# The projection's bias on VectorE, and the output's row sums from its last additions

## The chip, the core and the metric

The kernel runs on one core of one Trainium2 chip. The core has five engines that work side by side, each through its own list of instructions in a fixed order: TensorE (PE) multiplies matrices, VectorE (DVE) and ScalarE (ACT) do elementwise work and are the ones that carry matrix products out of PSUM, GpSimd (POOL) does elementwise work between SBUF tiles, and SyncE (SP) issues transfers. The metric is device time in microseconds (us) of one execution; smaller is better. Three runs of the kernel before took 2961.35, 2961.88 and 2963.93 us, so the median is 2961.88 us.

## The reference

Four graph layers, each followed by a layer norm of the sum of its input and its output, over 128 batches of 128 nodes with 512 features, all in 32-bit floats. The change is in layer 3, masked attention with eight heads, a projection with bias, and an inner layer norm:

```python
o = jnp.einsum('bhnm,bhmd->bhnd', attn, v).transpose(0, 2, 1, 3).reshape(b, n, d)
o = o @ w_proj + b_proj
mu = jnp.mean(o, axis=-1, keepdims=True)
var = jnp.mean(jnp.square(o - mu), axis=-1, keepdims=True)
ln = (o - mu) * jax.lax.rsqrt(var + LN_EPS) * ln_gamma + ln_beta
return o + ln
...
x = _layernorm(x + _L3_gnn_ref(x, ...), axis=-1)
```

So for each row the kernel needs `o` with its bias, the sum of `o` over the row (for the mean) and the sum of its squared deviations.

## The kernel before

**The planner.** The order of all engines' instructions is computed while the kernel is built. Each batch, and each product, is a Python generator (a chain) that asks for an engine with an estimated duration (`use("ACT", 0.48, ...)`), and `Plan.run` gives the engines out, one request at a time, by the earliest possible start, then by the request's order (`urgent`, `follow`) and the chain's rank, which mostly is the batch's number. `Plan.use` multiplies a duration by its engine's entry in `SLACK`. Instructions are issued in the order in which the planner grants them. A different duration, engine or constant anywhere therefore moves instructions of all engines against each other, in the whole kernel. The order of the instructions is fixed by this; the real start of each is fixed by semaphores on the chip.

**Buffers.** One arena of 100 units of 256 columns holds all the large tiles. A request can ask for a slot of a kind (`t` two units, `v`, `qk` and `xT` four). `CAPS` limits how many slots of a kind may be held at once: `xr`, the rows of x fetched again for the final sum, and `xT`, the transposed input of the layer-3 sections, are among them. The eight PSUM banks are handed out in the same way.

**Seven products for eight.** Large products of two blocks by two blocks are done by `seven` with seven block products (a Strassen-Winograd scheme). It accumulates on one PSUM bank `x`: after each step the partial sum is taken out to SBUF (`kept`), and the next matmul adds to the same bank, so TensorE cannot go on with this bank until the copy is done. The planner puts other matmuls in between. `kept` takes three partial sums out to where they are finished (ACT copies, line 943), `added` adds other banks onto them (DVE, `total`, line 937, or line 931 with `into`, which also writes the row sums through `accum_out`), and `last` takes out the fourth block (ACT, line 1025). In the inner section (`inner_section`, matmuls on line 892) `kept` adds on DVE instead (lines 950 and 952). `pair_product` (matmuls on line 1058) uses `seven` on pairs of batches: layer 0 with `into`, layer 1 without, and the projection of layer 3 (`projection`) without. `section` (matmuls on line 1111) uses it for q, k and v.

**The end of a batch.** After attention (`attends`, line 1212) ACT copies the heads' output (line 1457), and `projection` runs for two batches at a time, all but the last four batches. Then, for each batch, POOL adds the bias to the whole of `o` (`pool_add`, line 386, called on line 1468); `normed` has POOL add `o` to the fetched x (line 1540), ACT goes over `o` once to get its row sum (line 1560, `accum_out`), `statistics` turns the sum into the negative mean (DVE, line 357), the squared deviations (ACT, line 364) and the reciprocal root (POOL, line 321), and DVE makes the layer norm and the sum of the output (lines 1571 and 1576). The last `ENDS` = 8 batches take mean and variance with DVE's `bn_stats` (`mean_rstd`, line 308) instead. Batches before the last `KEPT` = 8 write x to DRAM (`spill`, line 1230) and fetch it again (`fetch`, line 1238), both through SP.

**The softmax.** Eight exponentials for each batch on ACT, one for each head (line 1407, each with an accumulator read); in the last `WHOLE` = 3 batches one ACT instruction over all heads instead (line 1401), with a subtraction and a sum on DVE beside it (lines 1397 and 1403).

Of the kernel before, what the change touches and what calls it, by code (L numbers as in the profile page):

```python
# [8 lines left out]
F32 = mybir.dt.float32  # L9
AF = mybir.ActivationFunctionType  # L10
ALU = mybir.AluOpType
# [4 lines left out]
P = 128  # L16
D = 512
K = D // P
G = 4
APART = 4  # L20
FIRST = 0
PAIRS = 2
SOON = (-4, 8, -4, 6, 10, 12)
WHOLE = 3
KEPT = 8
ATTENDS = 2
RUN = 5
SEVEN0 = 1
# [4 lines left out]
WAKE = 0.1  # L33
SWIFT = 0, 1, 2, 3, 4, 5
BEGIN = 1
ENDS = 8
INNER = 3
SEVEN1 = 1
SEVENP = 1
# [2 lines left out]
STICK = 0.6  # L42
CLOSE = 2900
SOFT = 8
PROJ = -3
SECTION = 22
PACE = 0
EAGER = 8
H = 8
# [7 lines left out]

UNITS = 100
UNIT = 256
CAPS = {"x": 8, "xr": 2, "yT": 11, "v": 5, "qk": 11, "xT": 6}  # L60
SIZES = {"u": 1, "t": 2, "x": 2, "early": 2, "xr": 2, "yT": 2, "v": 4, "qk": 4, "xT": 4}
LAST, AHEAD = 26, 0
DIRECT = 22
LATER = 2
LANDED = 2.2
LATE = 1.4
HANDOFF = {"PE": 0.2, "DVE": 0.13, "ACT": 0.16, "POOL": 0.09, "SP": 0.05}
DVE_ = 1.02
ACT_ = 1.08
POOL_ = 1.02  # L70
SP_ = 1.2
SLACK = {"PE": 1.0, "DVE": DVE_, "ACT": ACT_, "POOL": POOL_, "SP": SP_}
BORDERS = 0.1
# [170 lines left out]
def gnn_stack_kernel(  # L244
# [89 lines left out]

    def row_sums():

        n = small.tile([P, 6], F32, name="sums", bufs=20)
        return [n[:, c : c + 1] for c in range(6)]

    def layernorm_sums(xb, total, unread, pieces=1, total_out=None):  # L340
# [341 lines left out]
    class Group:  # L682


        def __init__(self, first, size):
            self.first, self.size, self.half = first, size, size // 2
            self.s = small.tile([P, G, 2], F32, name="s")
            self.logits = [Event(2) for _ in range(size // 2)]
            self.attention = [Event() for _ in range(size // 2)]
            self.landed, self.qk = Event(size), Event(8)  # L690
            self.have = {t: Event() for t in (T1, T2, T3, T4)}
            self.inner = {t: Event() for t in (I1, I2, I3, I4)}
            self.used = {t: Event(3) for t in (B11, B21)}
            self.squared = [Event() for _ in range(size)]
            self.valued = [Event(2) for _ in range(2)]
            self.rows, self.attended, self.scored = ([Event() for _ in range(size)] for _ in range(3))
            self.heads, self.o, self.sc, self.scratch = {}, {}, {}, {}
            self.eT, self.xT, self.slot, self.left = {}, {}, {}, {}
            self.qkT, self.v = {}, {}
            self.y, self.y_slot, self.mixed, self.turned, self.h = {}, {}, {}, {}, {}  # L700
            self.y0, self.mixed0, self.added0, self.biased, self.total = {}, {}, {}, {}, {}
            self.begun = [Event() for _ in range(3)]
            self.wide, self.dropped = Event(), Event()
            self.copied = [Event(2) for _ in range(size // 2)]
            self.projected = [[Event(2) for _ in range(2)] for _ in range(size // 2)]
            self.p, self.extra = [{} for _ in range(size // 2)], {}

        def block(self, t):

# [209 lines left out]
            adds=True, blocks=(B11, B21, B22, I1, I2, I3, I4),  # L919
        )  # L920

    def seven(rank, bx, wide, time, multiply, parts, finished, have, home, housed, slow=0.0, into=None, scale=None, adds=False, inner=None,
              blocks=(B11, B21, B22, T1, T2, T3, T4)):

        b11, b21, b22, t1, t2, t3, t4 = blocks
        copy, sum_ = {D: (0.45, 0.6), D // 2: (0.24, 0.33), P: (0.14, 0.2)}[wide]
        copy, sum_ = copy + slow, sum_ + slow

        def total(a, c, i, j):
            if into:  # L930
                nc.vector.scalar_tensor_tensor(  # L931
                    c, a, 1.0, c, op0=ALU.mult, op1=ALU.add, accum_out=into[j][i]
                )
            elif scale:
                nc.vector.scalar_tensor_tensor(c, a, scale, c, op0=ALU.mult, op1=ALU.add)
            else:
                nc.vector.tensor_tensor(c, a, c, op=ALU.add)  # L937

        def copied(c, a):
            if scale:  # L940
                nc.scalar.activation(c, a, AF.Identity, scale=scale)
            else:
                nc.scalar.copy(c, a)  # L943

        def kept(p, i, j, event):
            if into or adds:
                yield use("DVE", sum_, urgent=True)
                for a, c in parts(p, i, j):
                    if scale:
                        nc.vector.scalar_tensor_tensor(c, a, scale, c, op0=ALU.mult, op1=ALU.add)  # L950
                    else:
                        nc.vector.tensor_tensor(c, a, c, op=ALU.add)
                done(event)
                return
            got = yield use("ACT", copy, lambda: home(j), urgent=True)
            if got:
                housed(j, got)
            for a, c in parts(p, i, j):
                copied(c, a)
            done(event)  # L960

        def keep(p, i, j):
            event = Event()
            plan.start(kept(p, i, j, event), rank)
            return event

        def added(p, kept, i, j, event):
            yield kept
            yield use("DVE", sum_, urgent=True)
            for a, c in parts(p, i, j):  # L970
                total(a, c, i, j)
            finished(j)
            done(event)

        def add(p, kept, i, j):
            event = Event()
            plan.start(added(p, kept, i, j, event), rank)
            return event

        def release(event, bank):  # L980
            yield event
            give(bank)

        x = bank(bx, D)[:, :wide]
        multiply(x, A11, b11, True)
        m1 = keep(x, 0, 0)

        if inner:
            plan.start(inner(m1), rank)
        else:  # L990
            bz = yield use("PE", time, "ps")
            z = bank(bz, D)[:, :wide]
            multiply(z, A12, b21, True, True)
            plan.start(release(add(z, m1, 0, 0), bz), rank)

        yield m1
        yield have[t2]
        yield use("PE", time)
        multiply(x, S2, t2)
        u2 = keep(x, 1, 0)  # L1000

        yield have[t3]
        by = yield use("PE", time, "ps")
        y = bank(by, D)[:, :wide]
        multiply(y, S3, t3, True)
        yield u2
        yield have[t1]
        yield use("PE", time)
        multiply(x, S1, t1)
        u4 = keep(x, 1, 1)  # L1010
        c22 = add(y, u4, 1, 1)
        yield u4
        yield use("PE", time)
        multiply(x, S4, b22, final=True)

        def last(bx):
            if into or adds:
                yield use("DVE", sum_, urgent=True)
            else:
                yield use("ACT", copy, urgent=True)  # L1020
            for a, c in parts(x, 0, 1):
                if into or adds:
                    total(a, c, 0, 1)
                else:
                    copied(c, a)
            give(bx)
            finished(1)

        plan.start(last(bx), rank)
        yield c22  # L1030
        yield have[t4]
        yield use("PE", time)
        multiply(y, A22, t4, final=True)
        plan.start(release(add(y, u2, 1, 0), by), rank)
# [10 lines left out]
            nc.gpsimd.tensor_tensor(blocks(out), blocks(a), blocks(b), op=ALU.subtract)  # L1045
            done(have[t])

    def pair_product(rank, s, ready, blocks, release, out, finished, differed=None, into=None):

        yield ready  # L1050
        have = {t: Event() for t in (T1, T2, T3, T4)}
# [26 lines left out]
        def housed(j, slot):  # L1078
# [1 line left out]

        bx = yield use("PE", 0.87, "ps")
        yield from seven(
            rank, bx, D // 2, 0.87, multiply, parts, finished, have, home, housed, into=into,
        )

    def section(gr, s, before):
# [154 lines left out]
    def batch(i):  # L1241
# [218 lines left out]
        if SEVENP and gr.first + 2 * h < NB - PLAIN:  # L1460
            if h not in gr.extra:
                gr.extra[h] = None
                plan.start(projection(gr, h, i + PROJ), i + PROJ)
            done(gr.copied[h])
            yield gr.projected[h][b % 2]
            o, slot = gr.p[h][b % 2], gr.p[h]["slot", b % 2]
            biased = Event()
            plan.start(pool_add(o, bproj_sb, biased), i)
            yield biased
            yield from normed(i, o, lambda: give(slot), fetched)  # L1470
        else:
            yield from (last if i == NB - 1 else usual)(
                i, oT, v, lambda: gr.read(("v", b // 2), 2), fetched
# [35 lines left out]
    def projection(gr, h, i):  # L1509
# [20 lines left out]
        if gr.first + 2 * h + 2 == NB - PLAIN:  # L1530
            plan.start(again(), 0)
        yield from pair_product(
            i, 4, gr.copied[h], lambda t: t3 if t == T3 else v[:, t], release, gr.p[h],
            lambda j: done(gr.projected[h][j]), differed,
        )

    def add_rows(o, fetched, i):
# [12 lines left out]
        give(bp)  # L1550
        yield from normed(i, o, release, fetched)

    def normed(i, o, release, fetched):

        added = yield from add_rows(o, fetched, i)
        xb = xs[i]
        if i < NB - ENDS:
            total = row_sums()
            slot = yield use("ACT", 0.72, "t")
            nc.scalar.activation(buf(slot, D), o, AF.Identity, accum_out=total[0])  # L1560
            give(slot)
            nm, rstd, mean = yield from statistics(o, total, None)
            yield use("DVE", 0.07, urgent=True)
            nc.vector.tensor_scalar(mean, nm, -(D**0.5), None, op0=ALU.mult)
        else:
# [120 lines left out]
```

## Time and profile before

The profiled execution took 2960.8 us, with a span of 2959.0 us from the first to the last instruction, at a mean granted TensorE clock of 0.998.

| what | value |
|---|---|
| median of three runs | 2961.88 us |
| profiled execution, its span | 2960.8 us, 2959.0 us |
| ACT busy | 2052.8 us (69%) |
| POOL busy | 1894.8 us (64%) |
| DMA, mean over the span | 144 GB/s |
| PE busy, 100 to 2900 us, lowest and highest 100 us | 98.11 and 100.00 us |
| DVE busy, 100 to 2900 us, lowest and highest 100 us | 74.30 and 92.77 us |
| ACT copies of 128x256 on line 943 | 768, mean 368 ns |
| DVE adds of 128x256 on line 937 | 514, mean 414 ns |
| ACT row sums on line 1560 | 120, mean 623 ns, and 192 ns for each accumulator read |

An instruction count and a mean in a row of the profile cover one line and one shape. "Idle before" is the time in which the engine stood still just before instructions of the row, with the instruction that ended most of it. Matmul records are modelled at their ends: a 128x256 matmul is listed with 380 ns, though eight of them follow each other in 1.73 us, so a busy PE hides gaps shorter than the overlap.

### The profile page before, as it was taken

How to read it: one execution, taken by the hardware profiler on the slowest of the kernel's cores; microseconds unless marked ns; L12 is line 12 of the kernel's file. 1: busy time of each engine (PE TensorE's matmuls, PEld its weight loads, DVE VectorE, ACT ScalarE, POOL GpSimd, SP SyncE). 2: the span in 40 equal slices, each digit the busy share in tenths (PEclk: the TensorE clock that was granted, in tenths of full speed). 3: DMA queues.
4: the chain of work that ended last, by engine and by line, in shares of the span. 5: the costliest groups of instructions: out<-in, count | busy, mean ns of one | idle time of the engine just before them, and what ended most of it. 6: DMA issues, size and time to landing. Idle time of an engine off the chain costs nothing. (4 is left out here: it accounts for less than half of the span.)

```text
span 2959.0 us, 57327 instructions
## 1 busy us (share of the span) xinstructions
PE 2927.7 (99%) x17061; PEld 2476.9 (84%) x17061; DVE 2502.2 (85%) x7410; ACT 2052.8 (69%) x6211; POOL 1894.8 (64%) x2128
## 2 busy tenths in 40 slices
PE   9999999999999999999999999999999999999998
PEld 5688888888888888888888888888888888888886
DVE  7999888879888888888888788988878888878778
ACT  4657776667767577676767677677675786767675
POOL 4765757576666675665766666776666666666555
PEclk9999999999999999999999999999999999999999
DMA  6235745465455554554555465555446555544344
GB/s 221 83 90 154 191 118 172 109 183 131 128 159 152 148 158 118 162 149 127 169 129 164 115 172 144 160 150 152 132 130 177 141 145 152 148 123 122 107 140 128
DMA packets 861846, 425.40 MB, mean 144 GB/s; under 512 B 551008, under 2 KB 765024, under 8 KB 861536
## 3 DMA queue, kind: packets, MB, share of 16 engines
q1 hardware_dynamic: 843104, 388.18, 48.3%
q10 hardware_dynamic: 18432, 33.56, 3.0%
q8 instruction: 137, 2.24, 0.3%
q14 instruction: 173, 1.42, 0.2%
HBM read 219.68 MB, written 201.92 MB: 142 GB/s over the span
## 5 line engine op out<-in xcount | busy, mean ns | idle before, releaser
L1045 POOL TENSOR_TENSOR arena<-arena 128x256 f32<-128x256 f32 (+1 forms) x848 | 747.3, 887 | 383.9 <-ACT arena L1457 123.4
L321 POOL TENSOR_TENSOR sums<-sums,neghalf 128x1 f32<-128x1 f32 x631 | 417.8, 668 | 445.6 <-DVE sums L369 362.7
L943 ACT COPY arena<-ps 128x256 f32<-128x256 f32 (+1 forms) x892 | 340.8, 397 | 312.1 <-PE ps L1111 183.4
L1058 PE MATMUL ps<-wsum_sb,arena 128*128 128x256 f32 x2148 | 527.4, 380 | 3.3 <-ACT arena L943 1.9
L1058 PE MATMUL ps<-w_sb,arena 128*128 128x256 f32 x1872 | 462.6, 380 | 0.1
L1058 PEld LDWEIGHTS ps<-wsum_sb,arena 128*128 128x128 f32 x2148 | 398.9, 190 | 74.8 <-issue 14.6
L364 ACT ACTIVATE arena<-arena,sums 128x512 f32<-128x512 f32 x481 | 345.2, 718 | 130.3 <-DVE sums L357 84.3
L937 DVE TENSOR_TENSOR arena<-ps,arena 128x256 f32<-128x256 f32 (+2 forms) x824 | 315.1, 395 | 130.5 <-ACT arena L943 56.0
L1058 PEld LDWEIGHTS ps<-w_sb,arena 128*128 128x128 f32 x1872 | 346.1, 190 | 61.2 <-issue 16.5
L1407 ACT ACTIVATE arena<-arena,nmx 128x128 f32<-128x128 f32 x1000 | 391.1, 394 | 3.2 <-DVE nmx L1393 1.6
L1111 PE MATMUL ps<-arena,wqkv_sb 128*128 128x256 f32 (+1 forms) x1616 | 365.1, 371 | 0.0
L1111 PE MATMUL ps<-arena,wsum_sb 128*128 128x256 f32 (+1 forms) x1584 | 359.8, 373 | 0.0
L1111 PEld LDWEIGHTS ps<-arena,wqkv_sb 128*128 128x128 f32 x1616 | 293.7, 190 | 41.4 <-issue 4.8
L1111 PEld LDWEIGHTS ps<-arena,wsum_sb 128*128 128x128 f32 x1584 | 287.6, 190 | 43.1 <-issue 8.6
L347 ACT ACTIVATE arena<-arena,sums 128x512 f32<-128x512 f32 x255 | 205.1, 810 | 66.6 <-DVE sums L344 55.6
L1058 PE MATMUL ps<-wproj_sb,arena 128*128 128x256 f32 x992 | 236.1, 382 | 0.0
L386 POOL TENSOR_TENSOR arena<-arena,bproj_sb 128x512 f32<-128x512 f32 x124 | 159.7, 1302 | 111.6 <-ACT arena L943 102.8
L386 POOL TENSOR_TENSOR arena<-arena,beta_sb 128x512 f32<-128x512 f32 x128 | 174.5, 1370 | 79.3 <-DVE arena L1368 63.0
L1294 DVE SCALAR_TENSOR_TENSOR arena<-arena,wa_rows 128x512 f32<-128x512 f32 x256 | 210.3, 826 | 5.0 <-PE ps L1111 2.3
L1058 PEld LDWEIGHTS ps<-wproj_sb,arena 128*128 128x128 f32 x992 | 185.4, 190 | 28.9 <-issue 1.1
L1422 ACT ACTIVATE arena<-arena,rs 128x128 f32<-128x128 f32 x512 | 194.1, 396 | 5.2 <-DVE rs L1414 1.8
L1407 ACT ACTIVATION_READ_ACCUMULATOR arena<-arena,nmx 128x1 f32 x1000 | 191.0, 191 | 0.0
(143 smaller groups left out, 6026.2 us busy)
## 6 DMA issues: line engine op xcount, KB each, us to landing
p_d<-arena SPq DMA_DIRECT2D x256, 256.0 KB
arena<-p_d SPq DMA_DIRECT2D x128, 512.0 KB
x_d<-arena SPq DMA_DIRECT2D x234, 256.0 KB
arena<-x_d SPq DMA_DIRECT2D x936, 64.0 KB
arena<-in_x SPq DMA_DIRECT2D x127, 256.0 KB
out<-arena ACTq DMA_DIRECT2D x127, 256.0 KB
x_s<-arena SPq DMA_DIRECT2D x120, 256.0 KB
arena<-x_s SPq DMA_DIRECT2D x120, 256.0 KB
```

The lines of the kernel that those rows point to most:

```text
L321: nc.gpsimd.tensor_tensor(rstd, ve, neghalf, op=ALU.pow)
L347: nc.scalar.activation(xb, xb, AF.Identity, bias=nmr, scale=rstd)
L364: nc.scalar.activation(buf_or_bank(unread), xb, AF.Square, bias=nm, scale=D**-0.5, accum_out=var)
L386: nc.gpsimd.tensor_tensor(dst, dst, other, op=ALU.add)
L937: nc.vector.tensor_tensor(c, a, c, op=ALU.add)
L943: nc.scalar.copy(c, a)
L1045: nc.gpsimd.tensor_tensor(blocks(out), blocks(a), blocks(b), op=ALU.subtract)
L1058: nc.tensor.matmul(p, t[:, k], w[:, k, :], start=first and k == 0, stop=final and k == 1, skip_group_check=True,)
L1111: nc.tensor.matmul(to, lhs, rhs, start=first and j == 0 and k == 0, stop=final and k == 1, skip_group_check=True,)
L1294: nc.vector.scalar_tensor_tensor(unread, xb, 1.0, wa_rows[:, j, :], op0=ALU.mult, op1=ALU.mult, accum_out=gr.s[:, b, j : j + 1],)
L1407: nc.scalar.activation(pr[:, j, :], pr[:, j, :], AF.Exp, bias=nmx[:, j : j + 1], accum_out=sums[:, j : j + 1],)
L1422: nc.scalar.activation(pr[:, j, :], pr[:, j, :], AF.Identity, scale=rs[:, j : j + 1])
```

## The change

1. `seven` and `pair_product` take a `bias`, and `projection` passes `bproj_sb`. In `kept`, the three partial sums of a projection are now taken out by DVE, which adds the bias on the way, and no longer copied by ACT; `last` adds the bias on DVE too.
2. `projection` also passes `into`: the additions that finish a block write the row sums of its half through `accum_out`. `normed` gets these two half sums (`total`), and `statistics` adds them (line 359 before, `pieces` = 2).
3. POOL's pass over `o` for the bias, and ACT's pass over `o` for the row sum, are gone for the batches with a paired projection. `ENDS` is gone: all these batches use the sums, and only those that are not projected in pairs use `bn_stats`.
4. Constants of the planner: `APART` 4 to 5 (how many groups at the end schedule their attention product on its own), `WHOLE` 3 to 4, `KEPT` 8 to 6, `PROJ` -3 to -4 and `SECTION` 22 to 24 and `LATER` 2 to 3 (ranks), `LAST` 26 to 22 (without effect while `AHEAD` is 0), `CAPS` of `xr` 2 to 5 and of `xT` 6 to 5, the duration factors `DVE_` 1.02 to 1.04 and `POOL_` 1.02 to 1.06, and 24 buffers for `sums` where there were 20.

```diff
-APART = 4
+APART = 5
-WHOLE = 3
-KEPT = 8
+WHOLE = 4
+KEPT = 6
-ENDS = 8
-PROJ = -3
-SECTION = 22
+PROJ = -4
+SECTION = 24
-CAPS = {"x": 8, "xr": 2, "yT": 11, "v": 5, "qk": 11, "xT": 6}
+CAPS = {"x": 8, "xr": 5, "yT": 11, "v": 5, "qk": 11, "xT": 5}
-LAST, AHEAD = 26, 0
+LAST, AHEAD = 22, 0
-LATER = 2
+LATER = 3
-DVE_ = 1.02
+DVE_ = 1.04
-POOL_ = 1.02
+POOL_ = 1.06
...
-        n = small.tile([P, 6], F32, name="sums", bufs=20)
+        n = small.tile([P, 6], F32, name="sums", bufs=24)
...
+        def half_bias(i):
+            return bias[:, i * D // 2 : (i + 1) * D // 2]
+
-        def total(a, c, i, j):
+        def total(a, c, i, j, b=None):
             if into:
                 nc.vector.scalar_tensor_tensor(
-                    c, a, 1.0, c, op0=ALU.mult, op1=ALU.add, accum_out=into[j][i]
+                    c, a, 1.0, c if b is None else b, op0=ALU.mult, op1=ALU.add, accum_out=into[j][i]
                 )
...
-            if into or adds:
+            if into and bias is None or adds:
...
-            got = yield use("ACT", copy, lambda: home(j), urgent=True)
+            got = yield use(
+                *("ACT", copy) if bias is None else ("DVE", sum_), lambda: home(j), urgent=True
+            )
             if got:
                 housed(j, got)
             for a, c in parts(p, i, j):
+                if bias is not None:
+                    nc.vector.tensor_tensor(c, a, half_bias(i), op=ALU.add)
+                    continue
                 copied(c, a)
...
-                    total(a, c, 0, 1)
+                    total(a, c, 0, 1, None if bias is None else half_bias(0))
...
+                gr.sums[h] = [row_sums() for _ in range(2)]
+                gr.osum[h] = [(n[0], n[5]) for n in gr.sums[h]]
...
-            biased = Event()
-            plan.start(pool_add(o, bproj_sb, biased), i)
-            yield biased
-            yield from normed(i, o, lambda: give(slot), fetched)
+            yield from normed(i, o, lambda: give(slot), fetched, gr.sums[h][b % 2])
...
-            lambda j: done(gr.projected[h][j]), differed,
+            lambda j: done(gr.projected[h][j]), differed, into=gr.osum[h], bias=bproj_sb,
...
-    def normed(i, o, release, fetched):
+    def normed(i, o, release, fetched, total=None):
...
-        if i < NB - ENDS:
-            total = row_sums()
-            slot = yield use("ACT", 0.72, "t")
-            nc.scalar.activation(buf(slot, D), o, AF.Identity, accum_out=total[0])
-            give(slot)
-            nm, rstd, mean = yield from statistics(o, total, None)
+        if total:
+            nm, rstd, mean = yield from statistics(o, total, None, 2)
```

More of the change, by code (lines that the diff above doesn't have):

```diff
@@ L706, in __init__ @@
             self.p, self.extra = [{} for _ in range(size // 2)], {}
+            self.sums, self.osum = {}, {}
         def block(self, t):
@@ L920, in inner_section, with seven @@
         )
-    def seven(rank, bx, wide, time, multiply, parts, finished, have, home, housed, slow=0.0, into=None, scale=None, adds=False, inner=None,
+    def seven(rank, bx, wide, time, multiply, parts, finished, have, home, housed, slow=0.0, into=None, scale=None, adds=False, inner=None, bias=None,
               blocks=(B11, B21, B22, T1, T2, T3, T4)):
@@ L1046, in differences, with pair_product @@
             done(have[t])
-    def pair_product(rank, s, ready, blocks, release, out, finished, differed=None, into=None):
+    def pair_product(rank, s, ready, blocks, release, out, finished, differed=None, into=None, bias=None):
         yield ready
@@ L1082, in pair_product @@
         yield from seven(
-            rank, bx, D // 2, 0.87, multiply, parts, finished, have, home, housed, into=into,
+            rank, bx, D // 2, 0.87, multiply, parts, finished, have, home, housed, into=into, bias=bias,
         )
```

## The prediction

> **What bounds the kernel now.** I read the page first, then the chain of waits, then the waits by engine, and last the windows of 100 us. Busy times on the page:
>
> ```profile
> PE 2927.7 (99%) x17061; PEld 2476.9 (84%) x17061; DVE 2502.2 (85%) x7410; ACT 2052.8 (69%) x6211; POOL 1894.8 (64%) x2128
> ```
>
> PE is the bound, but matmul ends are modelled, so I count its work by its cadence. The chain of waits, here from 2600 to 2700 us (start, duration, what), runs almost wholly along PE:
>
> ```profile
> 2617.91 1.72 PE ps L420 x4
> 2640.40 1.73 PE ps L1111 x8
> 2642.99 1.99 PE ps L1191 x32
> 2644.98 3.64 PE ps L1212 x64
> 2662.89 1.78 PE ps L401 x16
> ```
>
> That gives 0.216 us for a matmul of 256 columns, 0.43 for 512, 0.111 for 128, and 0.062 and 0.057 for the two of attention. Times the counts of the groups by shape (9,532, 668, 2,726, 2,048 and 2,048) this is 2059 + 287 + 303 + 127 + 117 = 2893 us. The last matmul starts 2946 us into the span; what follows is batch 127's norm and store. So PE is off its cadence for at most 2946 - 2893 = 53 us, less some 10 us of small groups (the transposes at the start, the very last product): 43 us. How much of this is waiting for another engine stands in PE's waits (engine, line, what it waited for, us, times, longest):
>
> ```profile
> PE ps L1058 <- ACT arena L943: 1.9, 5, 0.5
> PE ps L1111 <- ACT arena L943: 1.9, 1, 1.9
> PE ps L393 <- ACT arena L1457: 1.8, 1, 1.8
> PE ps L393 <- ACT arena L412: 1.6, 1, 1.6
> PE ps L892 <- DVE arena L950: 1.4, 3, 0.7
> PE ps L892 <- DVE arena L952: 1.3, 4, 0.8
> PE ps L892 <- DVE sums L357: 1.3, 4, 0.6
> ...
> PE ps L1058 <- POOL arena L1045: 0.6, 1, 0.6
> ```
>
> All seventeen rows together are 17.8 us: ACT ends 8.2 of them (with 1.0 at L1348), DVE 6.8, POOL 2.0 (1.4 of it the identity at the start), DMA 0.8. That is all that a change off PE can win. The reader should see how small it is, and that the inner section (L892) pays most of DVE's part.
>
> **The change, part by part.** PE's list holds 8,544 entries in both programs, in the same shapes, so its work does not change. The other engines, by the order of the instructions of the two programs:
>
> ACT loses 248 copies of 128x256 out of PSUM (769 become 521) and 120 row sums. 248 x 0.368 = 91 us, 120 x (0.623 + 0.192) = 98 us. `WHOLE` turns eight exponentials of (0.394 + 0.191) into one of 1.06: -3.6; four batches that now use sums instead of `bn_stats` add one pass of squares each, 4 x 0.91 = +3.6. Sum -189: ACT goes from 2053 to 1864 us (63%).
>
> POOL loses its bias pass, 124 instructions, 159.7 us: 1895 to 1735 us (59%). The pass stood in the way of nothing but the output:
>
> ```profile
> L386 POOL TENSOR_TENSOR arena<-arena,bproj_sb 128x512 f32<-128x512 f32 x124 | 159.7, 1302 | 111.6 <-ACT arena L943 102.8
> ```
>
> The only instruction that waited for it is ACT's L1560, 0.2 us in all, so taking it off the output's latency is worth nothing on the end.
>
> DVE gains 186 `kept` adds with the bias; this form stands in the trace once the last batch is reached (0.41 us, shown below), so 186 x 0.414 = +77. It gains 62 `last` adds with a row sum, not in this shape with the bias in the trace; bounds are the same add without a sum, 0.414, and the add with a sum of layer 0 (L931), 0.415 + 0.082; I take the second, +31 (low end +26). 186 adds get an accumulator read: 186 x 0.083 = +15. Adding two half sums (L359, 0.202) in place of scaling one (L357, 0.142): 120 x 0.06 = +7. `WHOLE` +2.4, fewer `bn_stats` -2.1. Sum +131: DVE goes to 2633 us, 89% of the span. It gets something back. A DVE instruction with two SBUF inputs is sometimes held for as long as a POOL pass lasts:
>
> ```profile
> L1571 DVE SCALAR_TENSOR_TENSOR arena<-arena,sums,gamma_sb x120: 705/751/1808, 327.5 to 2896.0; 128x512 f32<-128x512 f32 x120
> 2946.91 0.41 DVE L1614 TENSOR_TENSOR arena<-ps,bproj_sb 128x256 f32<-128x256 f32 x1
> ```
>
> Minimum, median and maximum are 705, 751 and 1808 ns, against a mean of 904. Means over medians at L1294, L1571, L1576 and L1335 come to some 37 + 18 + 19 + 14 = 88 us, and the bias pass is about a tenth of POOL's two-input work (159.7 of some 1,500 us): -9 us. DVE also stood 7.9 us for L1560's sums and 36.2 us at adds of this shape for ACT copies; 186 of these 514 adds, 13 us, now follow an instruction of DVE itself. So 131 us of new work stand against some 30 us less of being held.
>
> One rule speaks against this. The Trainium skill (VectorE: DVE Perf Modes, Rules for kernel authors) says to minimise the number of DVE instructions, because fusing saves nothing in itself. The order has 250 DVE instructions more (6,659 to 6,909), and 371 fewer on ACT; the rule alone would price this as a loss of DVE time, and the row above agrees in sign (0.414 us on DVE for 0.368 on ACT). It would make the sum positive only if DVE set the time.
>
> Does it? Windows of 100 us (PE, PEld, DVE, ACT, POOL busy):
>
> ```profile
> 100.00:200.00 100.00, 98.28 (x456) 74.53 (x455) 92.77 (x313) 59.62 (x145) 68.41 (x76) 1.00 0.39 103
> 1800.00:1900.00 100.00, 99.53 (x566) 84.48 (x565) 90.51 (x276) 71.28 (x212) 72.34 (x83) 1.00 0.56 155
> 2700.00:2800.00 100.00, 100.00 (x680) 88.61 (x679) 74.30 (x198) 65.97 (x211) 53.23 (x63) 1.00 0.37 104
> ```
>
> The projections begin at 319 us (the first bias pass), so 131 us over 2600 us are 5 us per 100: 90.5 becomes 95.5. The fullest window, before 200 us, has no projection. So DVE does not run out anywhere, and PE at a DVE of 90.5 is 99.5% busy. That is the cover; if it is gone, the rival below is the price.
>
> Moved steps. `KEPT` = 6 adds two x_s writes and two reads of 256 KB: 4 issues of 0.39 us, 1.6 us of SP, and 1 MB on 425. SP stands 510 us for L1426 alone, so they are hidden; without that cover, 1.6 us behind which p_d reads of the last batches wait. `xr` 5 lets rows come earlier, `xT` 5 for 6 can make a `gather` wait for a slot. No PE wait on x_d is in the trace, and PE's waits at L1111 are 1.9 us; I take 0, between -1.9 and the rival's +15. In the tail the order has attention of 126 and 127 apart and each copied with nothing left to cover it, for 1.2 us each (0.58 of copy, two handoffs); now one such wait of 1.97 us is there. +0.4, taken as 0.
>
> Covers on one PSUM bank. Between an accumulation step and the next on its bank, the order leaves less than 1.2 us of PE work 48 times in projections, now 21; in inner products 57, now 46; layers 0 and 1, 31 and 32. Projections lose nothing at theirs now (no row of it), inner products some 0.07 us for each: -0.8.
>
> **Sum.** ACT-ended waits: bounds 0 and -6.6 (without 1.6 at the start); ACT has 21% more idle time and the copies in question are part of what leaves, so I take -5. POOL-ended -0.6. Covers -0.8. DVE-ended waits: bounds -6.8 and, if they grow as its idle time shrinks (457 to 326 us), +2.7; the less blocking and the greater load pull apart, I take 0. Sum -6.4 on the profiled 2960.8, so 2954.4; the median of the runs stood 1.1 above this execution, so 2955.5, given as 2955.
>
> **The rivals.** *Hidden anyway* (0.15): PE's 99% is untouched, ACT and POOL were not the bound, and the new order has its own waits of the same size: 2961.9, within 4. For it: the waits are scattered, most under 0.8 us. Against it: ACT's are the largest. *DVE takes over the waits* (0.25): inner steps (L950, L952) queue behind new DVE adds, in each of 31 groups. The waits at L892 average some 0.36 us; one more of 0.5, a new DVE add with its sum, in each group is +15.5: 2977, and from 0.2 a group on it eats the gain. It decides once DVE is late by more than the inner step's cover, whose median in the order is 2.2 us. For it: DVE at 89%, and PE's DVE-ended waits are nearly all there. Against it: stages at 90.5 lose little. *All named waits go*: 2961.9 - 16 = 2946, the edge of the forecast.
>
> **The numbers.** About 0.2%, 5.9 us, is what a measurement of this kernel can tell from no change. Forecast 0.60, own range 2946 to 2960: 0.45 of it below 2956, 0.15 within. Hidden anyway 0.15, all within. DVE 0.25, of it 0.23 slower. So faster 0.45, same 0.32, slower 0.23. The range 2945 to 2972 takes in all but the upper half of the DVE rival and the far edge of the forecast.
>
> **What would show it.** PE's waits after should lack most rows that end in ACT L943; DVE busy near 2620, ACT near 1864, POOL near 1735; the last matmul near 2940 us. L892's rows by DVE grown past 15 us would show the rival, and PE waiting for x_d landings the `xT` cap. A time under 2943 would mean that PE's unnamed gaps moved too, which I leave out.

## The result and the profile after

The changed kernel takes 2969.03 us (median of ten runs, 2967.90 to 2972.25), the kernel before in the same session 2961.61 (ten runs, 2959.61 to 2963.93). The ratio is 1.0029 [1.0021, 1.0038]: 0.29% slower, outside the 0.2% that can be told from no change. The forecast was 2955 and faster, so its sign was wrong; the time lies inside the range.

In the listings after, lines have moved by a few: 1058 is now 1066, 1111 is 1119, 1191 is 1199, 892 stays, 401 is 400, 420 is 419, 931 is 934, 937 is 940, 952 is 955, 943 is 946, 357 is 356 (one sum) or 358 (two half sums), 386 is 385, 1571 is 1574. New is 965, the three kept partial sums of a projection, taken out by DVE with the bias. The page's busy times:

```profile
PE 2931.8 (99%) x17061; PEld 2477.8 (83%) x17061; DVE 2560.6 (86%) x7908; ACT 1907.1 (64%) x5716; POOL 1710.4 (58%) x2004
```

PE has the same 17,061 records, and ACT and POOL are lighter by 146 and 184 us. DVE is heavier by 58. The chain of waits still runs along PE, and its cadence is the old one (start, duration, what):

```profile
2607.51 1.73 PE ps L1119 x8
...
2617.01 0.86 PE ps L419 x2
...
2626.49 1.99 PE ps L1199 x32
```

Eight matmuls of 256 columns still take 1.73 us and 32 of attention 1.99. What changed is PE's waits (engine, line, what it waited for, us, times, longest):

```profile
PE ps L1066 <- DVE arena L965: 4.8, 6, 1.6
PE ps L1356 <- ACT arena L349: 3.7, 7, 1.3
PE ps L892 <- DVE arena L955: 3.5, 5, 1.3
PE ps L1602 <- ACT arena L1465: 2.2, 1, 2.2
PE ps L892 <- DVE sums L368: 1.8, 3, 0.9
PE ps L571 <- POOL ident masks.py:199: 1.4, 1, 1.4
PE ps L1119 <- POOL arena L1053: 1.3, 2, 1.0
PE ps L1066 <- DVE arena L955: 1.2, 2, 0.9
```

All rows together are 25.7 us, where they were 17.8. DVE ends 14.0 of them (6.8 before), ACT 8.8 (8.2), POOL 2.7 (2.0), DMA 0.2 (0.8). The new add of line 965 is the largest row; the steps of line 955 pay 4.7 in two rows (3.5 in the inner section, 1.2 in layer 0), where line 952 paid 1.7 before (1.3 and 0.4). By the matmul that waits, DVE's part rose at the pair products (0.4 to 7.0) and hardly in the inner section, L892 (5.4 to 5.6). The rows that end in the copies of the large products shrank as forecast, and others that end in ACT came in their place (L349, L1465).

The profiled execution of the changed kernel took 2972.25 us, the slowest of its ten, so compare its stages and not its length. Its last matmul starts 2958.4 us into the span, 12.4 us later than before; 12.1 us follow it (12.9 before), so what follows the last matmul is not the place. Against the cadence (0.216, 0.43 and 0.1115 us for matmuls of 256, 512 and 128 columns, 0.062 and 0.057 in attention) the starts of all matmuls leave 57.4 us of gaps, 45.1 before: those of at least 0.18 us sum to 31.2 us (23.9 before), shorter ones to 18.2 (15.5), and those around attention to 8.0 (5.6). So some six tenths of the 12.4 us lie in gaps of the length of the named waits. Stages of 100 us (PE, PEld, DVE, ACT, POOL busy, then granted clock, DMA share, GB/s):

```profile
100.00:200.00 100.00, 97.13 (x450) 73.60 (x449) 92.06 (x291) 59.16 (x143) 68.99 (x76) 1.00 0.39 102
600.00:700.00 100.00, 99.55 (x600) 87.35 (x599) 93.95 (x294) 74.67 (x238) 59.22 (x66) 1.00 0.56 153
2700.00:2800.00 100.00, 99.70 (x667) 85.90 (x666) 80.43 (x241) 62.08 (x192) 53.55 (x65) 1.00 0.45 124
```

DVE's fullest stage stands at 93.95, and PE is 99.55% busy in it. No engine has run out: the loss is a handful of single events. One of them, with the records of DVE, POOL and PE around it (start, duration, what; in brackets idle before):

```profile
2181.00 0.42 DVE L965 TENSOR_TENSOR arena<-ps,bproj_sb 128x256 f32<-128x256 f32 x1
...
2181.78 1.27 POOL L385 TENSOR_TENSOR arena<-arena,bias_sb 128x512 f32<-128x512 f32 x1
...
2181.83 1.49 DVE L788 SCALAR_TENSOR_TENSOR arena<-arena 128x256 f32<-128x256 f32 x1
...
2183.25 0.68 DVE L1359 TENSOR_REDUCE mx<-ps 128x1 f32<-128x512 f32 x1
...
2184.21 0.42 DVE L965 TENSOR_TENSOR arena<-ps,bproj_sb 128x256 f32<-128x256 f32 x1
...
2184.68 0.70 PE L1066 MATMUL ps<-wsum_sb,arena 128*128 128x256 f32 x2 [1.62 <-DVE arena L965]
```

Line 788 is a two-input instruction of DVE with a median of 0.42 us. Here it starts 0.05 us after a POOL pass of 128x512 and ends 0.27 us after it, 1.07 us longer than its median. The reduction behind it follows late, then the add of line 965, and PE, which needs the bank that this add frees, stands for 1.62 us. Before the change the same kind of step was a copy in ACT's queue and did not stand behind DVE's instructions.

### The profile page after: what moved, and what is told of

Same layout as the page of the kernel before. It is cut to its first block, busy times and chain, and to the rows that moved or that the text cites. A ratio compares the mean times of both kernels' runs of the same rounds, so it can differ in the third digit from the quotient of the medians.

```text
span 2970.5 us, 57212 instructions
## 1 busy us (share of the span) xinstructions
PE 2931.8 (99%) x17061; PEld 2477.8 (83%) x17061; DVE 2560.6 (86%) x7908; ACT 1907.1 (64%) x5716; POOL 1710.4 (58%) x2004
## 3 DMA queue, kind: packets, MB, share of 16 engines
q14 instruction: 173, 1.42, 0.2%
## 4 chain that ended last, share of the span: by engine, by line
PE 82%; DVE 12%; issue 1%; DMA 1%; POOL 1%; ACT 1%; SPq 0%; ACTq 0%; DVEq 0%; POOLq 0%
PE ps L1066 30%; PE ps L1119 29%; PE ps L400 4%; PE ps L1199 4%; PE ps L892 4%; PE ps L1220 4%; PE ps L1356 3%; PE ps L419 2%; PE ps L392 2%; DVE arena L934 1%; DVE arena L1434 1%; DVE arena L1424 1%; DVE arena L1579 1%; DVE arena L1574 1%; DVE nmx L1401 1%
## 5 line engine op out<-in xcount | busy, mean ns | idle before, releaser
L1053 POOL TENSOR_TENSOR arena<-arena 128x256 f32<-128x256 f32 (+1 forms) x848 | 736.3, 873 | 501.4 <-PE ps L1066 136.7
L1066 PE MATMUL ps<-wsum_sb,arena 128*128 128x256 f32 x2148 | 533.9, 381 | 6.1 <-DVE arena L965 4.8
L946 ACT COPY arena<-ps 128x256 f32<-128x256 f32 (+1 forms) x644 | 250.0, 409 | 363.7 <-PE ps L1119 203.4
L1415 ACT ACTIVATE arena<-arena,nmx 128x128 f32<-128x128 f32 x992 | 385.1, 391 | 27.7 <-DVE nmx L1401 26.0
L1066 PEld LDWEIGHTS ps<-w_sb,arena 128*128 128x128 f32 x1872 | 346.7, 191 | 58.7 <-issue 12.7
L940 DVE TENSOR_TENSOR arena<-ps,arena 128x256 f32<-128x256 f32 (+2 forms) x638 | 239.0, 388 | 114.9 <-ACT arena L946 50.4
L385 POOL TENSOR_TENSOR arena<-arena 128x512 f32<-128x512 f32 x129 | 169.1, 1316 | 132.2 <-DVE arena L934 124.5
L1430 ACT ACTIVATE arena<-arena,rs 128x128 f32<-128x128 f32 x512 | 184.2, 392 | 9.0 <-DMA arena<-x_d 3.0
```

The costliest lines, as they stand in the source:

```text
L385: nc.gpsimd.tensor_tensor(dst, dst, other, op=ALU.add)
L1066: nc.tensor.matmul(p, t[:, k], w[:, k, :], start=first and k == 0, stop=final and k == 1, skip_group_check=True,)
L1415: nc.scalar.activation(pr[:, j, :], pr[:, j, :], AF.Exp, bias=nmx[:, j : j + 1], accum_out=sums[:, j : j + 1],)
L1430: nc.scalar.activation(pr[:, j, :], pr[:, j, :], AF.Identity, scale=rs[:, j : j + 1])
```

## The experiments

The suspects, all of which would show as waits ended by DVE:

- **A**: adds on DVE make PE wait, in whatever order the work runs.
- **B**: the retuned constants are the worse part.
- **C**: every new order draws its own scattered waits, and the order of before is a low draw.
- **D**: steps that free PSUM queue behind DVE instructions that a POOL pass holds; copies on ACT do not.
- **E**: it is the sums, not the bias.

Two kinds of kernel are used. In some, the planner makes a new order. In the others ("old plan", "new plan") what the planner books is left untouched, and only the instruction issued at a booked place differs, so TensorE's list and order are exactly those of the base kernel. Ratios are to the kernel before, run in the same session.

### Code alone, constants alone

```diff
-APART, WHOLE, KEPT, PROJ, SECTION, LATER = 5, 4, 6, -4, 24, 3
+APART, WHOLE, KEPT, PROJ, SECTION, LATER = 4, 3, 8, -3, 22, 2
...
-DVE_, POOL_, CAPS xr, xT = 1.04, 1.06, 5, 5
+DVE_, POOL_, CAPS xr, xT = 1.02, 1.02, 2, 6
```

This is the code-alone kernel against the changed one, with the assignments and the two `CAPS` entries put together here; the other kernel is the kernel before with the opposite edit.

> The changed code with all planner constants of before. Theory A (the adds on VectorE make TensorE wait, whatever the order): about +7 us on before, ratio 1.002 to 1.004, and PE's waits that DVE ends near 14 us as in the changed kernel. Theory B (the retuned constants made a worse order, the code itself costs nothing): within 2 us of before, and DVE-ended waits near 7 us. Theory C (every new order draws its own waits): anywhere between -5 and +12 us, not at the same value as the changed kernel.

> The code of before with the new planner constants; ACT copies and POOL's bias pass stay. Theory A: within 2 us of before. Theory B: +7 us, as the changed kernel. Theory C: anywhere between -5 and +12 us.

Measured: code alone 2974.96 us, 1.0046 [1.0033, 1.0058]; constants alone 2979.44, 1.0058 [1.0044, 1.0072]. Each half is slower than both together (1.0029), so the two do not add, and neither is the culprit. The second is the more telling one: it has the old code, with ACT's copies, and PE's waits rose from 17.8 to 31.8 us, 19.3 of them ended by DVE, mostly at steps that the change never touched:

```profile
PE ps L892 <- DVE arena L952: 5.8, 11, 0.8
PE ps L892 <- DVE sums L357: 3.2, 5, 1.1
```

More waits ended by DVE thus come from a new order alone.

### The old plan with the new instructions

```diff
             for a, c in parts(p, i, j):
+                if bias is not None:
+                    nc.vector.tensor_tensor(c, a, half_bias(i), op=ALU.add)
+                    continue
                 copied(c, a)
```

The fourth block is taken out by DVE as well, POOL's bias pass is left out, and in the first of the two kernels the additions write the sums and ACT's row-sum pass is left out; the second keeps ACT's pass.

> TensorE's order and the plan of before, kept instruction for instruction; only where the planner had an ACT copy of a projection's partial sum, VectorE adds the bias instead, the additions write the row sums, and POOL's bias pass and ACT's row-sum pass are left out of the lists. Theory A: +5 to +15 us, because DVE's list was not planned for 248 more instructions. Theories B and C: within 3 us of before, since the order is the same; below before by 2 us or more if the freed ACT and POOL were worth something.

> The plan and TensorE's order of before; the projection's four blocks take the bias on VectorE and POOL's bias pass is left out, but ACT keeps its row-sum pass and its place. Theory D (an evacuation on VectorE queues in order behind VectorE instructions that POOL's passes hold, an ACT copy does not): nearly all of the 28 us of the run with both parts, 2983 to 2990 us, with 18 to 22 us of PE's waits at the line of the DVE bias add. Theory E (it is the additional sums): 2962 to 2970 us.

Measured: 2990.18 us, 1.0099 [1.0085, 1.0113], and 2987.79, 1.0094 [1.0079, 1.0109]. Nearly all of it is the moved bias, which both have; the sums add some 2 us, each kernel taken against the kernel before in its own session. In the first kernel:

```profile
PE ps L1076 <- DVE arena L969: 21.3, 30, 1.5
PE ps L894 <- DVE sums L357: 2.8, 6, 1.3
```

(Line 1076 is the matmul of pairs, line 969 the new add.) Put into DVE's queue at places that were booked for ACT, the 186 adds cost some 21 us in 30 waits; planned for DVE, they cost 4.8 in 6. So A is right for an order that does not know of them, and the planner removes three quarters of it.

### The new plan with the copies back on ACT

```diff
-                    nc.vector.tensor_tensor(c, a, half_bias(i), op=ALU.add)
+                    nc.scalar.copy(c, a)
```

The bias is left out of the three kept blocks here.

> TensorE's order and the plan of the changed kernel; only the three partial sums of each projection are copied out by ACT instead of being added to the bias by VectorE (the bias is left out of these three blocks). Theory A: the 4.8 us of waits at line 965 vanish and most of the rise with them, so 2962 to 2964 us. Theory B and C: the order keeps its waits, 2967 to 2970 us, with the waits at the projection ended by ACT copies instead.

Measured: 2973.73 us, 1.0042 [1.0030, 1.0055], beside 1.0029 for the changed kernel: no gain at all. The waits changed hands:

```profile
PE ps L1066 <- ACT arena L965: 4.9, 15, 0.8
PE ps L1356 <- ACT arena L349: 4.0, 6, 1.3
```

The total is 23.9 us: DVE's part falls to 6.7, ACT's rises to 14.3. Six waits of up to 1.6 us on DVE became fifteen of up to 0.8 on ACT, in an order that had booked DVE. So at this order the copies on ACT are no cheaper, and A's forecast of 2962 to 2964 us failed. But the order had been planned for DVE, so this run does not show that the adds cost nothing: taking them off DVE removed 7.3 us of its waits, and ACT, which was not planned for, gave 5.5 back.

### Neutral constants

```diff
-WAKE = 0.1
+WAKE = 0.11
```

The same for `LATE` 1.4 to 1.42 and `BORDERS` 0.1 to 0.105, each alone, in the kernel before and in the changed one. `WAKE` is the planner's price for starting TensorE after it stood idle, `LATE` its factor on the delays of transfers, and `BORDERS` its price for a change between attention and other matmuls: no instruction changes, only the order.

> The kernel before with one constant of the planner's model moved from 0.10 to 0.11 us (the start of TensorE after idling). No instruction is added or taken; only the order changes, from TensorE's 288th entry on. Theory C (each order draws its own waits, and the one of before is a low draw): 5 to 20 us slower than before. Theory A (the change costs by what it does): within 3 us of before.

> The kernel before with the factor of transfer delays in the planner moved from 1.40 to 1.42: another order of the same instructions. Theory C: 5 to 20 us slower than before, and not by the same amount as the other constant. Theory A: within 3 us of before.

> The kernel before with the planner's price of a change between attention and other matmuls moved from 0.100 to 0.105 us. Theory C (each order draws its own waits): 2963 to 2985 us. If the kernel before is typical of its code: within 3 us of before.

> The changed kernel with the same constant moved from 0.10 to 0.11. Theory C: somewhere from 2965 to 2985 us, most likely above the changed kernel's 2969, since that one too was a chosen order. Theory A: within 3 us of 2969.

> The changed kernel with the factor of transfer delays moved from 1.40 to 1.42. Theory C: somewhere from 2965 to 2985 us, not the same as with the other constant. Theory A: within 3 us of 2969.

> The changed kernel with the same price moved from 0.100 to 0.105 us. Theory C: 2965 to 2985 us. If the 7 us are the cost of what the change does: within 3 us of 2969, and the new orders of the code of before near 2962.

Measured, with the two halves of the change as a fifth order of each code (waits of PE in the profile, us, and of them those ended by DVE):

| order | old code, us | waits (DVE) | new code, us | waits (DVE) |
|---|---|---|---|---|
| as it is | 2961.6 | 17.8 (6.8) | 2969.0 | 25.7 (14.0) |
| `LATE` 1.42 | 2963.7 | 21.1 (12.4) | 2980.4 | 31.0 (11.9) |
| `WAKE` 0.11 | 2983.9 | 34.5 (12.4) | 2972.1 | 22.9 (12.1) |
| `BORDERS` 0.105 | 2997.6 | 37.9 (22.9) | 2978.2 | 32.4 (12.7) |
| the other's constants | 2979.4 | 31.8 (19.3) | 2975.0 | 27.8 (14.7) |
| mean of five | 2977.2 | | 2974.9 | |

A price changed by 1 to 10% moves the old code by 2, 22 and 36 us in the order of the rows, and the new one by 11, 3 and 9. Both originals are the fastest of their five. Every order but the original of the old code has at least 11.9 us of waits ended by DVE: the 14.0 of the changed kernel is ordinary, and the 6.8 of the kernel before is the exception. That is C.

The waits at the new adds themselves (L965) depend on the order as well. Here they are for the new code with the old constants, with `BORDERS` 0.105 and with `LATE` 1.42; with `WAKE` 0.11 there is no such row at all:

```profile
PE ps L1066 <- DVE arena L965: 3.3, 2, 3.1
PE ps L1066 <- DVE arena L965: 2.0, 4, 0.8
PE ps L1066 <- DVE arena L965: 1.0, 3, 0.5
```

The 4.8 us of the changed kernel are the most of its code's five orders, and the order with none takes 2972.1 us: the adds do not cost that amount by what they are.

The means differ by 2.3 us in favour of the new code, with standard deviations of 14.9 and 4.6, so five orders can't tell the codes apart.

### Parts of the change at the old order

First POOL's bias pass alone is left out, and the bias with it; then this and ACT's row sum with the adds writing the sums, ACT's copies kept (the fourth block on DVE with the bias, the other three blocks without it).

```diff
-        nc.gpsimd.tensor_tensor(dst, dst, other, op=ALU.add)
+        if other is not bproj_sb:
+            nc.gpsimd.tensor_tensor(dst, dst, other, op=ALU.add)
...
+                nc.vector.scalar_tensor_tensor(
+                    c, a, 1.0, c, op0=ALU.mult, op1=ALU.add, accum_out=osum[j][i]
+                )
```

> The plan and TensorE's order of before, with only POOL's pass for the projection's bias left out (the bias is left out of the paired projections). If the gain of the run with the sums is POOL's pass, which holds VectorE: 2957 to 2959 us. If it is ACT's row-sum pass: 2961 to 2963 us.

> The plan and TensorE's order of before; ACT keeps the copies of the partial sums, the additions write the row sums, the last block is taken out by VectorE with the bias and a sum, POOL's bias pass and ACT's row-sum pass are left out (the bias is left out of three of the four blocks). Theory D: 2958 to 2966 us, since nothing that TensorE waits for has moved. Theory E: 2975 us or more.

Measured: 2956.61, 0.9985 [0.9976, 0.9994], and 2958.04, 0.9991 [0.9982, 1.0000]. The 160 us of POOL's pass are worth some 4 us of time, and the sums by the adds, which remove ACT's pass (98 us by its rows), give nothing on top. To see the sums apart, POOL's pass was kept, and the sum of the bias, made once by a reduction, was added to each row sum:

```diff
+        nc.vector.tensor_reduce(sumb, bproj_sb, axis=AX.X, op=ALU.add)
...
+                    nc.scalar.activation(c, a, AF.Identity, accum_out=osum[1][0])
...
+            nc.vector.tensor_scalar(total[5], total[5], sumb, None, op0=ALU.add)
```

> A version that could beat both: the plan and TensorE's order of before, ACT keeps all copies (the last block's with a row sum), the additions write the row sums, ACT's row-sum pass is gone, POOL keeps the bias pass, and the sum of the bias is added to the row sum by one small VectorE instruction. If ACT's pass was worth something: 2957 to 2960 us. If only POOL's pass was: 2960 to 2964 us, no gain.

> The same version as before it (the sums from the additions, ACT's row-sum pass gone, POOL's bias pass kept, the plan of before), with the one sum over the bias moved from the first instructions, where it made TensorE wait 14 us near 50 us of the span, behind the sums of the projection's weights. If ACT's pass is worth something: 2957 to 2960 us. If only POOL's pass was: within 2 us of before, and no gain over it.

The first try, 2979.77 us, 1.0066 [1.0054, 1.0079], says nothing of the sums: its reduction stands in DVE's queue near the start, in front of layer 0. DVE stood 14.4 us there until the bias had landed, and PE had one wait of 14.1 us, from 35 to 49 us. With the reduction behind the sums of the weights it is 2964.91, 1.0012 [1.0003, 1.0021]. So at this order the exchange of ACT's 120 row sums (98 us by their rows) for sums on DVE gains nothing and costs 2.7 us net. E may supply that much; it is not the bulk of what the kernels of the old plan lost, and falls as the main cause.

### POOL's 128x512 passes

D says that holds by POOL hurt more where DVE frees PSUM, so without these passes the changed order should gain more. All additions of `pool_add` (those of `bias_sb`, `beta_sb` and, in the kernel before, `bproj_sb`, and the sum with x; 507 in the kernel before, 383 in the changed one, and two of 256 columns) are left out of the computation, at both orders. POOL's block sums of line 1045, 124 of them 512 wide, stay.

```diff
-        nc.gpsimd.tensor_tensor(dst, dst, other, op=ALU.add)
```

> The plan and TensorE's order of the changed kernel, with POOL's passes of 128x512 left out (layer 0's bias, beta of layer 3, and the sum of x and o), so that POOL holds VectorE less often. Theory D: PE's DVE-ended waits fall from 14 us to 9 or less and the time by 4 to 8 us, to 2961 to 2965. Theory C alone (the waits are in the order, whoever holds whom): within 2 us of 2969.

> The plan and TensorE's order of before, with all of POOL's passes of 128x512 left out (layer 0's bias, beta of layer 3, the projection's bias, and the sum of x and o). Theory D: PE's waits fall less than in the changed order, since fewer of its evacuations are on VectorE: 1 to 4 us below before. Theory C alone: within 2 us of before.

Measured: the changed order 2955.97, 0.9987 [0.9978, 0.9997], 13.1 us below its base; the old order 2944.72, 0.9946 [0.9931, 0.9961], 16.5 below its own. The page of the latter:

```profile
PE 2921.5 (99%) x17061; PEld 2477.4 (84%) x17061; DVE 2410.5 (82%) x7410; ACT 2052.0 (70%) x6211; POOL 1211.1 (41%) x1619
```

DVE issues the same 7,410 records as before and is busy 92 us less: that is what these passes held it for. PE's waits fall from 17.8 to 9.1 us, those ended by DVE from 6.8 to 3.2. At the changed order they fall from 25.7 to 17.0, and from 14.0 to 4.6. POOL's passes cost more than the whole change, but both orders pay for them: the changed one more in waits ended by DVE (9.4 against 3.6), not in time. The old order also loses 124 passes more, those of the bias, which are worth some 4 us by the run above; without them the two gains are much the same. As the reason for the difference between the two kernels D fell. These two runs do not show that all of the gain comes through holds: the named waits account for 8.7 us of it at each order, and whatever waited for the results of the passes is freed too.

### Halves instead of whole passes

If a hold lasts as long as the pass, a shorter pass holds for less, and here what waits for the results still has to wait. The kernel before, with each POOL addition of 128x512 issued as two of 128x256 at the same booked place:

```diff
-        nc.gpsimd.tensor_tensor(dst, dst, other, op=ALU.add)
+        wide = dst.shape[-1]
+        for c in (slice(0, wide // 2), slice(wide // 2, wide)):
+            nc.gpsimd.tensor_tensor(dst[:, c], dst[:, c], other[:, c], op=ALU.add)
```

> The kernel before in its own order, with each of POOL's 128x512 additions issued as two of 128x256. If VectorE is held until the POOL instruction in progress ends, a hold lasts half as long: 2 to 6 us below before, and the maximum at DVE's L1571 near 1.2 us where it was 1.8. If the holds last as long as POOL works at all: no gain, and 2 to 5 us slower, since 509 more instructions on POOL add some 0.1 us each.

Measured: 2955.33 us beside 2962.25, 0.9979 [0.9970, 0.9988]: faster than both kernels. The page, and line 788 of before (now 790; minimum, median, maximum in ns):

```profile
PE 2926.4 (99%) x17061; PEld 2479.1 (84%) x17061; DVE 2477.4 (84%) x7410; ACT 2053.3 (70%) x6211; POOL 1995.6 (68%) x2637
```

```profile
L790 DVE SCALAR_TENSOR_TENSOR arena<-arena x64: 381/424/934, 48.8 to 2718.8; 128x256 f32<-128x256 f32 x64
```

The maximum was 1376 before and is 934, with nearly the same median (422 and 424); DVE is busy 25 us less, and PE's waits are 14.2 us with 3.3 ended by DVE (17.8 and 6.8). POOL pays 101 us for it and has the room. Not as expected: the maximum of the layer norm (line 1573) stays at 1795 ns, and its mean only falls from 904 to 887. One form of 512 columns is left on POOL (line 1047, 124 with a mean of 1382 ns), and the longest instruction of line 1573, at 1618.9 us, starts 0.02 us after one of these.

## Why the prediction was wrong

**PE's work unchanged: right.** Same records, same cadence.

**ACT and POOL lighter: right in direction, ACT's size wrong.** POOL was forecast at 1735 us and measured 1710. ACT was forecast at 1864, 189 lighter, and measured 1907, 146 lighter. The forecast added up rows, and ACT's records overlap: at the old order the 248 copies, 91 us by their rows, take 67.5 us off its busy time (2053.1 us without POOL's bias pass, 1985.6 with the bias moved as well), and the 120 row sums, 98 by their rows, 72.8 (1985.6 to 1912.8). In time, ACT's row sums are worth nothing at that order, as argued, but POOL's pass is worth 4 us [1.8 to 7.1, by its interval], where the sum had 0.6 for POOL and let the shorter holds on DVE cancel against its greater load.

**DVE heavier by 131: the mechanism right, the size wrong.** It is 58. The rows themselves do add up to the forecast: 76.6 us for line 965, 30.6 for the fourth block, 89.2 more for additions with a sum and their reads, 75.7 less for additions without, 8.5 more for the means: 129. But a row's duration is not what DVE gives up. Over all its records DVE grew by 107 us, and 48 of these overlap another record, which busy time counts only once: two such adds in a row start 0.33 us apart, and the 37.5 us of accumulator reads take nearly nothing. The means of lines 788, 1294, 1571 and 1576 also fell (586 to 524 ns, 826 to 818, 904 and 907 to 868), some 15 us of shorter holds, while line 1335's rose (792 to 812, 3 us); 9 us of shorter holds were forecast.

**No stage where DVE runs out: right.** 93.95 at most, 95.5 forecast.

**The tail at nothing: nearly right.** 12.1 us follow the last matmul, 12.9 before; ahead of it PE waits 2.2 and 0.7 us for copies of the last heads, where it waited 1.8 before. (The prediction's 1.97 is the duration of the matmuls in front of that wait, whose row says 1.75.)

**The sum: the step that failed.** Its terms "ACT-ended waits ... I take -5", "POOL-ended -0.6", "DVE-ended waits ... I take 0" treat PE's waits of before as a fixed list from which a lighter engine strikes rows. Measured: ACT-ended +0.6, POOL-ended +0.7, DVE-ended +7.2, against the forecast's 0 and its upper bound of +2.7. The list does not survive a new order. The struck rows went, and others of the same size came, as the neutral constants show on code that nobody touched: 3 to 20 us more of waits from a changed price alone. The prediction's "new order has its own waits of the same size" stood in the rival *hidden anyway*, but at zero net cost; the order of before was a low draw, 16 us below the mean of its five, so a new draw was likelier to cost than to gain. Nothing in one profile shows that; it takes a second order.

**The rival *DVE takes over the waits*** had the sign and the engine, but not the place: it put the waits into the inner section, whose rows by DVE stayed (5.4 to 5.6 us), and they grew at the pair products (0.4 to 7.0), 4.8 of it at the new adds themselves. Its price, +15.5, was twice the +7.4 measured. That the new adds cost this by what they are is not shown: in the other four orders of the new code they make PE wait 0 to 3.3 us, the old code has 12.4 to 22.9 us of waits ended by DVE in its four other orders, and the changed order with copies on ACT is no faster. What the adds themselves cost was seen only where they were not planned for: 2987.8 us, 31 above the kernel that leaves out POOL's pass alone.

What stays open: whether the change is worth anything over many orders. Five of each give -2.3 us with a standard error of 7. And of the 12.4 us by which the last matmul moved, the named waits cover 7.9; the other 4.5 lie in short gaps and around attention, and no row assigns them.

## What to carry to other kernels

Where an order is worked out by a planner, compare a change at a frozen order, or over several orders made by neutral edits, before putting a small difference down to the code: here neutral edits moved the time by 2 to 36 us, and the change by 7. A step that frees PSUM inherits what stands ahead of it in its engine's queue, holds by another engine's passes among them, so ask that of the engine before moving it, and not the mean of its row alone. Before setting aside an engine that is off the path, look at what it holds up: leaving out POOL's additions gained 13 to 17 us, though POOL was busy 64% and 58% of the span, and issuing them as halves, with more work in all, gained 7.

## What the runs showed of the hardware

**An accumulator read on DVE takes hardly any slot.** An add of 128x256 with a sum is listed as 0.415 us and 0.082 us for the read, one without as 0.414. From start to start, back to back, they take 0.341 and 0.334 us. In the layer norm's second step the read and the next instruction start together:

```profile
2952.15 0.08 DVE L1579 DVE_READ_ACCUMULATOR arena<-arena,sums 128x1 f32 x1
2952.15 0.75 DVE L1579 SCALAR_TENSOR_TENSOR arena<-arena,sums 128x512 f32<-128x512 f32 x1
```

**A hold lasts for the other engine's pass.** In the kernel before, 22 of the 64 instructions of line 788 and 42 of the 127 of line 1571 last over 1.25 times the median of their line, and each of these overlaps a POOL instruction. With the additions of `pool_add` gone, line 788's maximum falls from 1376 to 959 ns, with halves to 934. The Trainium skill (GPSIMD Engine Reference, Specifications) says that POOL shares its SBUF interfaces with VectorE and names VectorE instructions with two SBUF inputs among those that contend; the rows agree.

**The clock can drop after a short wait.** In the kernel before with `BORDERS` 0.105, PE waits 5.4 us from 634.2 us on and 2.7 us from 847.6 on; the granted clock is 0.5 from 639.3 on for 3.4 us, and from 850.9 on for 10.2 us, three times as long. The waits, then two stretches (PE, PEld, DVE, ACT, POOL busy, clock, DMA share, GB/s):

```profile
PE ps L420 <- DVE arena L788: 5.4, 1, 5.4
PE ps L1058 <- DVE arena L952: 4.9, 5, 2.7
```

```profile
840.00:850.00 10.00, 6.86 (x29) 5.01 (x27) 5.19 (x14) 4.24 (x10) 8.58 (x12) 1.00 1.01 283
850.00:862.00 12.00, 10.25 (x24) 6.96 (x24) 7.78 (x26) 2.41 (x8) 4.08 (x5) 0.57 0.31 68
```

In the second stretch the mean clock is 0.57, and matmuls of 256 columns start 0.427 us apart at the lower clock, for 0.216 elsewhere. Neither the kernel before nor the changed one has such a stretch in mid-run, so it is no part of their difference, but it makes a bad order dearer than its waits. The Trainium skill (TensorE: Matmul & The Clock Gate, Part 1) gives a free-running window of about 3.4 us after which an idle TensorE runs at half rate; the length agrees, while with `LATE` 1.42 drops of 3.4 us follow waits of only 2.0 us in both codes (at 967 us in the old one, at 727 us in the new), and waits of 2.3 and 2.4 us in the same kernels bring none.
